# A recurrent layer with sixteen experts: solve steps in batches of eight tiles, gram products nine tiles ahead

## The chip, the core and the metric

The kernel runs on one core of one Trainium2 chip. The metric is the device time of one launch in microseconds. The engines are TensorE (PE: matmuls, written to PSUM), VectorE (DVE), ScalarE (ACT), GpSimd (POOL) and SyncE (SP), which here issues all DMAs. Each engine works through its own queue in order and waits for others by semaphores.

## What is computed

The input x is 8 sequences of 1024 steps of 256 numbers. Two branches work on the normalized input and are multiplied:

```python
xn = _layernorm(x, axis=-1)
# s: W is updated step by step, all 8 sequences together
def step(W, inp):
    xt, vt = inp                       # vt = xt @ Wkv[d:].T + bkv[d:]
    y = xt @ W.T
    gW = scale * ((y - vt).T @ xt)     # scale = 2 / (b * d)
    return (W - eta * gW, y)
# f: 16 experts, the gates of the best 6, made to sum to one
for e in range(E):
    out = out + x @ expert_w[e] * gate[:, e:e + 1]
x = x + s * _silu(f)
```

## The kernel before

A **tile** is 16 time steps of 8 sequences, 128 rows; there are 64 tiles (NT). Within a tile the recurrence is solved at once: with the products of all rows with each other (the gram matrix), masked and scaled into a triangular matrix a, the kernel finds u, the inverse of a unit triangular matrix, and so the errors of all rows against the state at the tile's start. Then the state W goes to the next tile. All large products are float32 numbers split into a high and a low part, three matmuls each (`accumulate`, L242 on); `split` (L142) makes the parts, the high one on ScalarE (L143), the low one on VectorE or GpSimd (L144).

Per tile i these functions run:

- `load` and `layernorm`: x comes by DMA; st, mv (VectorE), ve, rstd (GpSimd), then xn: on ScalarE with a shift for the first 8 tiles (`BY_ACT`, L206), on VectorE after that (L208). From tile 4 on a transposed copy is made by 32x32 blocks (xr, L214), written to a DRAM tile (`bounce`) and read back by four DMAs as xT.
- `transpose_x`: splits xT into xT_two (L235 on) and xn into xn_hi and xn_lo (L238 to L240).
- `project` and `project_end`: the gram products (two matmuls at L256, the copy cross on ScalarE at L262, and one more at L274, which adds the transposed cross part), and vr, the target values and router logits together (six matmuls). Of these come xx and a (L279, L280), lg (L269) and hv (L282).
- `gates`, for a group of tiles: the best six of sixteen logits, and the gates.
- `solve_0` to `solve_6`, for a group of tiles: small matmuls of 32x32 and 64x64 for all tiles of the group, with copies between them on VectorE and ScalarE. `solve_0` makes q1 on VectorE (L414). Then come six steps on TensorE, each of which needs the results of the one before: q and uq (L402), z (L440, L444), y (L458), z2 (L473), y2 (L484). At the end u is split into u_hi and u_lo.
- `errors_1`, `errors_2`, `update`: the recurrence of tile i, in order: pe with the state wt, p and its parts, pe with u, step, then wt_ps and the next state.
- `experts`, for each of eight pairs of experts: six matmuls of 512 columns into h (three PSUM buffers), and the weighted sum: for six experts (`ON_ACT`) on ScalarE and GpSimd (part, L554; mix, L557), for the rest on VectorE (mix, L563, L565). `finish` multiplies the branches and sends the tile out.

The order on TensorE and SyncE is written out by hand (`manual_schedule`); a scheduler places the instructions of the others. The main loop goes over 64 tiles and eight pairs each: a pair slot is numbered 8 i + pair, and `events` (L610 on) lists what is put ahead of the expert matmuls of each slot. Tiles are grouped 1, 1, 2, and then by four (`counts`, L89); a group serves for gates and solve steps both. With f the first slot of a group's first tile, its solve steps stand at f-10, f-8, f-6, f-4, f-2 and f (L635). Gram and vr of tile i stand at 8 (i - 5) + 1 (`AHEAD`), their ends one slot later, the first tiles earlier by a list (`preps`, L638). `errors_2` stands at 8 i + 3, `update` at 8 i + 5, or + 6 for every fourth tile (L622).

Of the kernel before, what the change touches and what calls it, by code (L numbers as in the profile page):

```python
# [36 lines left out]
P = 128  # L37
# [6 lines left out]
GROUP = 4  # L44
AHEAD = 5
BY_PE = 4
BY_ACT = 8
# [4 lines left out]
def ttt_moe_kernel(  # L52
# [26 lines left out]
    prep = ctx.enter_context(tc.tile_pool(name="prep", bufs=AHEAD + 1))  # L79
# [13 lines left out]
    for n, c in enumerate(counts):  # L93
        where += [(n, sum(counts[:n]), j) for j in range(c)]

# [27 lines left out]
    r_raw = const.tile([NE, D], F32)  # L123
    nc.sync.dma_start(out=r_raw, in_=router_w)
    w_raw = const.tile([P, 2 * KD, D], F32)
# [65 lines left out]
    def layernorm(i):  # L191
# [10 lines left out]
        q.xn = work.tile([P, D], F32, tag="xn", name=f"xn_{i}", bufs=3)  # L202
# [10 lines left out]
        xr = work.tile([P, D], F32, tag="xr", name=f"xr_{i}")  # L213
# [12 lines left out]
    def transpose_x(i):  # L226
        q = tiles[i]
        q.xT_two = prep.tile([P, KD, 2, P], F32R, tag="xT_two", name=f"xT_two_{i}")
        q.xT_hi, q.xT_lo = q.xT_two[:, :, 0, :], q.xT_two[:, :, 1, :]
        if i < BY_PE:  # L230
            t = misc(f"xtr_{i}")
            for k in range(KD):
                nc.tensor.transpose(t[:, k * P : (k + 1) * P], q.xn[:, k * P : (k + 1) * P], ident)
            split(q.xT_hi, q.xT_lo, t[:, : KD * P].rearrange("p (k t) -> p k t", k=KD))
        else:  # L235
            hi, lo = (a.rearrange("p k (b t) -> p k b t", b=NQ) for a in (q.xT_hi, q.xT_lo))
            split(hi, lo, q.xT.rearrange("p (b k t) -> p k b t", b=NQ, k=KD))
        q.xn_hi = prep.tile([P, D], F32R, tag="xn_hi", name=f"xn_hi_{i}")  # L238
        q.xn_lo = prep.tile([P, D], F32R, tag="xn_lo", name=f"xn_lo_{i}")
        split(q.xn_hi, q.xn_lo, q.xn, nc.gpsimd)  # L240
# [10 lines left out]
    def project(i, g, j):  # L251
# [10 lines left out]
        nc.scalar.copy(q.cross, gram[:, P : 2 * P])  # L262
        vr = misc(f"vr_{i}")
# [6 lines left out]
        q.vr = vr  # L270

    def project_end(i, g, j):
        q = tiles[i]
        nc.tensor.matmul(  # L274
            q.gram[:, :P], lhsT=q.cross, rhs=ident_r, start=False, stop=True, skip_group_check=True
        )
        xx = work.tile([P, P], F32, tag="xx", name=f"xx_{i}")
        with tc.high_priority() if j == g.count - 1 else nullcontext():
            nc.vector.tensor_add(xx, q.gram[:, :P], q.cross.bitcast(F32))  # L279
            nc.vector.tensor_mul(g.a[:, j, :, :], xx.unsqueeze(1).broadcast_to([P, 2, P]), masks)  # L280
        q.hv = prep.tile([P, D], F32, tag="hv", name=f"hv_{i}")
        nc.vector.scalar_tensor_tensor(  # L282
            q.hv, q.vr[:, :D], -0.5, half_b, op0=ALU.mult, op1=ALU.subtract
        )
# [15 lines left out]
    ones = const.tile([P, P], F32)  # L300
    nc.gpsimd.memset(ones, 1.0)
    keep = const.tile([P, 2, P], F32)
# [12 lines left out]
    u_full, t_half = [], []  # L315
    for n in range(2):
        u = const.tile([P, GROUP, P], F32, tag=f"u_{n}", name=f"u_{n}")
        nc.gpsimd.memset(u, 0.0)
        u_full.append(u)
        t = const.tile([P, GROUP // 2, P // 2], F32, tag=f"t_{n}", name=f"t_{n}")  # L320
        nc.gpsimd.memset(t, 0.0)
        t_half.append(t)

    stores = {}

    def open_group(n, first, count):
        m, j = first // GROUP, first % GROUP
        if j == 0:
            store = stores[m] = Prepared()
            store.a = group.tile([P, GROUP, 2, P], F32, tag="a", name=f"a_{m}")  # L330
            store.lg = group.tile([P, GROUP, NE + 2], F32, tag="lg", name=f"lg_{m}")
            nc.gpsimd.memset(store.lg[:, :, NE:], ABSENT)
            store.u, store.t = u_full[m % 2], t_half[m % 2]
            store.u_hi = group.tile([P, GROUP, P], F32R, tag="u_hi", name=f"u_hi_{m}")
            store.u_lo = group.tile([P, GROUP, P], F32R, tag="u_lo", name=f"u_lo_{m}")
            for name in ("q1", "q2", "uq", "tq", "z"):
                setattr(store, name, group.tile([P, GROUP, Q], F32, tag=name, name=f"{name}_{m}", bufs=1))
            store.z2 = group.tile([P, GROUP // 2, P // 2], F32, tag="z2", name=f"z2_{m}", bufs=1)
        g = Prepared()
        g.n, g.first, g.count = n, first, count  # L340
        for name, t in vars(stores[m]).items():
            if name in ("t", "z2"):
                setattr(g, name, t)
            else:
                setattr(g, name, t[:, j : j + count])
# [6 lines left out]
        g.half_of = [((j + n) % 2, (j + n) // 2) for n in range(count)]  # L352
        return g

    def gates(g):
# [35 lines left out]
        for j in range(c):  # L391
            q = tiles[g.first + j]
            q.gate, q.eps_sum = gate[:, j, :], eps_sum[:, j : j + 1]
            q.u_hi, q.u_lo = g.u_hi[:, j, :], g.u_lo[:, j, :]

    def step_q(g, name, rhs, out):
# [3 lines left out]
        for j in range(c):  # L400
            for b in range(P // Q):
                nc.tensor.matmul(  # L402
                    ps[at(b), j * Q : (j + 1) * Q], lhsT=g.a[at(b), j, 0, at(b)],
# [7 lines left out]
    def solve_0(g):  # L411
        c = g.count
        for b in range(P // Q):
            nc.vector.tensor_add(  # L414
                g.q1[at(b)], g.a[at(b), :, 1, at(b)],
                ident_q[at(b), :].unsqueeze(1).broadcast_to([Q, c, Q]),
# [17 lines left out]
    def solve_3(g):  # L434
        c = g.count
        ps = solving(f"z_ps_{g.n}")
        for j in range(c):
            o = slice(j * Q, (j + 1) * Q)
            for a, b in ((0, 1), (2, 3)):
                nc.tensor.matmul(  # L440
                    ps[at(a), o], lhsT=g.a[at(b), j, 0, at(a)], rhs=g.uq[at(b), j, :],
# [3 lines left out]
                ps[at(1), o], lhsT=g.a[at(0), j, 1, at(1)], rhs=g.tq[at(0), j, :],  # L445
# [24 lines left out]
    def solve_5(g):  # L470
        ps = solving(f"z2_ps_{g.n}").rearrange("p (m h) -> p m h", h=H)
        for j, (odd, m) in enumerate(g.half_of):
            nc.tensor.matmul(  # L473
                ps[at(odd, H), m, :], lhsT=g.a[H:, j, 0, :H], rhs=g.u[H:, j, H:],
                start=True, stop=True, skip_group_check=True,
            )
        for odd, js, ms in [(None, None, slice(0, g.count // 2))] if g.count == GROUP else g.halves:
# [3 lines left out]
    def solve_6(g):  # L481
# [8 lines left out]
        split(g.u_hi, g.u_lo, g.u)  # L490
# [4 lines left out]
    def errors_1(i):  # L495
# [8 lines left out]
        q.p = work.tile([P, D], F32, tag="p", name=f"p_{i}")  # L504
# [3 lines left out]
        q.p_hi = work.tile([P, D], F32R, tag="p_hi", name=f"p_hi_{i}")  # L508
        q.p_lo = work.tile([P, D], F32R, tag="p_lo", name=f"p_lo_{i}")
        split(q.p_hi, q.p_lo, q.p)  # L510

    def errors_2(i):
# [3 lines left out]
        q.step_hi = work.tile([P, D], F32R, tag="step_hi", name=f"step_hi_{i}")  # L516
        nc.scalar.mul(q.step_hi, e, neg_c)  # L517
        q.step_lo = work.tile([P, D], F32R, tag="step_lo", name=f"step_lo_{i}")
# [3 lines left out]
        q.hy = work.tile([P, D], F32, tag="hy", name=f"hy_{i}")  # L522
# [47 lines left out]
    def finish(i):  # L570
# [9 lines left out]
        o = work.tile([P, D], F32, tag="o", name=f"o_{i}")  # L580
# [7 lines left out]
    opened = {}  # L588
# [10 lines left out]
    def project_y(i):  # L599
        n, first, j = where[i]  # L600
        project_end(i, opened[n], j)
        if j == counts[n] - 1:
            with tc.high_priority():
                solve_0(opened[n])

    def solve_x(n, m):
        solve[m](opened[n])
# [25 lines left out]
    for n, c in enumerate(counts):  # L633
        f = 8 * sum(counts[:n])
        spots = solves.get(n, (f - 10, f - 8, f - 6, f - 4, f - 2, f))  # L635
        for m, spot in enumerate(spots):
            put(spot // 8, spot % 8, solve_x, n, m)
    preps = {1: 6, 2: 10, 3: 12, 4: 17, 5: 19, 6: 25, 7: 27, 8: 33, 9: 35}  # L638
    for i in range(1, NT):
        spot = preps.get(i, 8 * (i - AHEAD) + 1)  # L640
        norm, turn = {1: (1, 4), 2: (7, 9), 3: (8, 8)}.get(i, (spot - 10, spot - 1))
        fetch = max(4, spot - 21)
        if i >= BY_PE:
# [3 lines left out]
        put(spot // 8, spot % 8, project_x, i)  # L647
        put((spot + 1) // 8, (spot + 1) % 8, project_y, i)
# [3 lines left out]
    transpose_x(0)  # L652
    split_experts(0)
    load(1)
    for e in range(4, NE):
# [3 lines left out]
        if e in (9, 11):  # L659
            load(2 if e == 9 else 3)  # L660
    project_x(0)
    project_y(0)
# [41 lines left out]
```

## Time and profile before

| | us |
|---|---|
| median of 3 runs | 998.58 (998.12 to 998.90) |
| span of the profiled execution, first to last instruction | 997.4 |
| mean granted TensorE clock | 0.995 |
| TensorE busy | 974.0 |
| VectorE busy | 770.1 |
| GpSimd busy | 444.4 |
| ScalarE busy | 438.2 |

The profile is of one execution, whose own time the page gives as the span alone. A row of the timeline gives the start and the length of an instruction or of a merged run, the engine, the line, what it writes and reads, and how many (x). Matmuls overlap, so the length of one is more than the distance to the next; distances are read from starts. A float32 matmul that isn't split (the small ones of the solve steps) leaves two records. A row by stage gives for each engine the busy time and, behind it in brackets, the instructions; then the clock granted to TensorE, the share of the DMA engines and GB/s.

### The profile page before, as it was taken

What the parts mean: (1) busy time and instruction counts of PE and PEld (TensorE: products, weight loads), DVE (VectorE), ACT (ScalarE), POOL (GpSimd) and SP (SyncE); (2) the same over time, 40 slices, a digit from 0 to 9 for tenths busy, and PEclk for the clock granted to TensorE, in tenths of its full rate; (3) what the DMA queues carried; (4) which work ended last, traced back from release to release, by engine and by line L of the source; (5) the groups of instructions that cost most, each with busy time, mean ns of one, the idle gap of its engine ahead of it and who ended that gap; (6) DMA issues with size and microseconds to landing.
All of it is one profiled execution on the core that took longest, in us unless ns stands there. A gap on an engine that the chain in (4) does not pass through costs nothing.

```text
span 997.4 us, 19643 instructions
## 1 busy us (share of the span) xinstructions
PE 974.0 (98%) x6672; PEld 799.4 (80%) x6672; DVE 770.1 (77%) x2225; ACT 438.2 (44%) x1182; POOL 444.4 (45%) x677
## 2 busy tenths in 40 slices
PE   5899999999999999999999999999999999999997
PEld 4678888888888888888888888888888888888785
DVE  6878796877878778796877878778797777877664
ACT  6544444353443534444353443534444353443432
POOL 6633444444345344444444345344444444344343
PEclk9899999999999999999999999999999999999999
DMA  8021111111111111111111111111111111110000
GB/s 238 15 62 38 39 26 44 39 26 43 39 28 43 38 28 43 38 28 43 38 28 43 38 28 43 30 36 44 38 28 43 38 28 43 33 28 12 12 12 11
DMA packets 67092, 38.65 MB, mean 39 GB/s; under 512 B 38176, under 2 KB 66992, under 8 KB 66992
## 3 DMA queue, kind: packets, MB, share of 16 engines
q1 hardware_dynamic: 66992, 37.41, 13.8%
q8 instruction: 52, 0.85, 0.4%
q14 instruction: 48, 0.39, 0.1%
HBM read 21.13 MB, written 16.25 MB: 37 GB/s over the span
## 4 chain that ended last, share of the span: by engine, by line
PE 91%; DVE 3%; ACT 2%; issue 1%; POOL 1%; DMA 1%; SPq 0%; POOLq 0%; DVEq 0%; ACTq 0%
PE h L247 70%; PE pe L247 6%; PE wt_ps L247 5%; PE vr L247 5%; PE gram L256 2%; PE gram L274 1%; DVE q L414 1%; PE q_ps L402 1%; PE z_ps L473 1%; PE y_ps L484 1%; PE y_ps L458 1%; DVE mix L565 1%; PE uq_ps L402 1%; PE z_ps L440 0%; DMA eta_sb<-in_L_attn_eta_dram 0%
## 5 line engine op out<-in xcount | busy, mean ns | idle before, releaser
L247 PE MATMUL h<-we,xT_two 128*128 128x512 f32 x3072 | 784.8, 401 | 4.5 <-DVE mix L565 2.7
L247 PEld LDWEIGHTS h<-we,xT_two 128*128 128x128 f32 x3072 | 553.6, 188 | 121.0 <-issue 2.9
L565 DVE SCALAR_TENSOR_TENSOR mix<-h,gate,mix 128x256 f32<-128x256 f32 x576 | 265.8, 476 | 96.4 <-PE h L247 67.2
L554 ACT ACTIVATE part<-h,gate 128x256 f32<-128x256 f32 x384 | 181.9, 474 | 302.5 <-DVE mix L565 153.9
L557 POOL TENSOR_TENSOR mix<-mix,part 128x256 f32<-128x256 f32 x256 | 189.5, 740 | 115.7 <-ACT part L554 104.7
L579 POOL TENSOR_TENSOR my<-m,hy 128x256 f32<-128x256 f32 x64 | 47.6, 744 | 161.0 <-DVE m L575 157.6
L557 POOL TENSOR_TENSOR mix<-part,part 128x256 f32<-128x256 f32 x64 | 49.9, 780 | 74.0 <-ACT part L554 74.0
L582 POOL TENSOR_TENSOR o<-o,x 128x256 f32<-128x256 f32 x63 | 46.4, 737 | 67.7 <-DVE lg L269 58.0
L195 DVE BATCH_NORM_STATS2 st<-x 128x6 f32<-128x256 f32 x64 | 27.0, 423 | 58.2 <-DMA x<-in_L_attn_x_dram 58.2
L199 POOL TENSOR_SCALAR ve<-mv 128x1 f32<-128x1 f32 x64 | 14.9, 234 | 100.6 <-DVE mv L197 67.9
L247 PE MATMUL vr<-w_vr,xT_two 128*128 128x272 f32 x384 | 59.1, 290 | 0.0
L144 DVE TENSOR_TENSOR wt_lo<-wt_ps,wt_hi 128x512 fp32r<-128x512 f32 x64 | 42.9, 670 | 21.0 <-ACT wt_hi L143 20.8
L143 ACT CAST p_hi<-p 128x256 fp32r<-128x256 f32 x64 | 26.0, 406 | 68.9 <-DVE p L505 68.7
L208 DVE TENSOR_SCALAR xn<-x,mv,rstd 128x256 f32<-128x256 f32 x56 | 45.2, 808 | 11.9 <-POOL rstd L201 11.8
L143 ACT CAST xT_two<-xT 128x256 fp32r<-128x256 f32 x60 | 24.4, 407 | 65.4 <-PE h L247 63.8
L247 PEld LDWEIGHTS vr<-w_vr,xT_two 128*128 128x128 f32 x384 | 52.3, 191 | 0.0
L517 ACT ACTIVATE step_hi<-pe,neg_c 128x256 fp32r<-128x256 f32 x64 | 30.3, 474 | 46.3 <-PE pe L247 46.0
L144 POOL TENSOR_TENSOR xn_lo<-xn,xn_hi 128x256 fp32r<-128x256 f32 x64 | 47.8, 749 | 6.0 <-ACT xn_hi L143 5.4
L247 PEld LDWEIGHTS pe<-wt_hi,xT_two 128*128 128x128 f32 x256 | 39.2, 188 | 5.8
L144 DVE TENSOR_TENSOR p_lo<-p,p_hi 128x256 fp32r<-128x256 f32 x64 | 40.4, 631 | 0.8 <-ACT p_hi L143 0.4
L247 PE MATMUL pe<-wt_hi,xT_two 128*128 128x256 f32 x256 | 40.7, 281 | 0.0
L143 ACT CAST wt_hi<-wt_ps 128x512 fp32r<-128x512 f32 x64 | 37.1, 580 | 6.8 <-PE wt_ps L247 6.4
(117 smaller groups left out, 1197.6 us busy)
## 6 DMA issues: line engine op xcount, KB each, us to landing
x<-in_L_attn_x_dram SPq DMA_DIRECT2D x64, 128.0 KB, 2.7
out_dram<-o SPq DMA_DIRECT2D x64, 128.0 KB, 2.3
bounce<-xr SPq DMA_DIRECT2D x60, 128.0 KB, 2.3
xT<-bounce SPq DMA_DIRECT2D x240, 32.0 KB, 1.8
raw<-in_L_ffn_expert_w_dram SPq DMA_DIRECT2D x16, 256.0 KB, 5.2
w_raw<-in_L_attn_Wkv_dram SPq DMA_DIRECT2D x1, 256.0 KB, 2.7
w_raw<-in_L_attn_W_dram SPq DMA_DIRECT2D x1, 256.0 KB, 5.1
bias<-in_L_attn_bkv_dram SPq DMA_DIRECT2D x1, 128.0 KB, 4.8
```

The source lines that it names most:

```text
L143: nc.scalar.copy(hi, src)
L144: (engine or nc.vector).tensor_sub(lo, src, hi.bitcast(F32))
L195: nc.vector.bn_stats(st, xt)
L208: nc.vector.tensor_scalar(q.xn, xt, mv[:, 0:1], rstd, ALU.subtract, ALU.mult)
L247: nc.tensor.matmul(o, lhsT=a, rhs=b, start=first and m == 0, stop=(m == len(terms) - 1), **kw)
L256: nc.tensor.matmul(gram[:, : 2 * P], lhsT=q.xT_hi[:, k, :], rhs=q.xT_two[:, k, :, :].rearrange("p n t -> p (n t)"), start=(k == 0), stop=( ...
L517: nc.scalar.mul(q.step_hi, e, neg_c)
L554: nc.scalar.mul(part, he, gate)
L557: nc.gpsimd.tensor_add(new, q.mix[1], part)
L565: nc.vector.scalar_tensor_tensor(new, he, gate, q.mix[j], op0=ALU.mult, op1=ALU.add)
L579: nc.gpsimd.tensor_mul(my, m, q.hy)
L582: (nc.vector if i == NT - 1 else nc.gpsimd).tensor_add(o, o, xt)
```

## The change

Gates stay with the groups of four. The solve steps get batches of their own: 1, 1, 2, 4, 4, 4, then six of eight tiles. The gram products leave `project` and become `products`, which stands nine tiles ahead (`FAR`) instead of five; vr stays at five. The splitting of xn leaves `transpose_x` and becomes `split_x`, two tiles ahead of its update. ScalarE normalizes the first 24 tiles instead of 8. Buffers are counted anew: more for xn (10) and xT_two (11), three groups' worth of a, and single buffers for p, p_hi, p_lo, step_hi, step_lo, hy, xr, xx, u_hi, u_lo and the u that the steps build; some constants of the start share buffers with later tiles, and o is made in place of my. With f the first slot of a batch's first tile, the steps of a batch of eight stand at f-11, f-9, f-7, f-5, f-3 and f-1.

```diff
+BATCH = 8
 AHEAD = 5
+FAR = 9
-BY_ACT = 8
+BY_ACT = 24
...
-    prep = ctx.enter_context(tc.tile_pool(name="prep", bufs=AHEAD + 1))
+    prep = ctx.enter_context(tc.tile_pool(name="prep", bufs=FAR + 2))
...
+    batches = [1, 1, 2, 4, 4, 4]
+    while sum(batches) < NT:
+        batches.append(min(BATCH, NT - sum(batches)))
...
+    def split_x(i):
+        q = tiles[i]
+        q.xn_hi = prep.tile([P, D], F32R, tag="xn_hi", name=f"xn_hi_{i}", bufs=3)
+        q.xn_lo = prep.tile([P, D], F32R, tag="xn_lo", name=f"xn_lo_{i}", bufs=3)
         split(q.xn_hi, q.xn_lo, q.xn, nc.gpsimd)
...
+    u_full = const.tile([P, BATCH, P], F32)
+    nc.gpsimd.memset(u_full, 0.0)
...
-    def solve_0(g):
-        c = g.count
+    def solve_0(g, lo, hi):
+        first = (g.first + lo) % GROUP
+        a = grams[(g.first + lo) // GROUP][:, first : first + hi - lo]
         for b in range(P // Q):
             nc.vector.tensor_add(
-                g.q1[at(b)], g.a[at(b), :, 1, at(b)],
-                ident_q[at(b), :].unsqueeze(1).broadcast_to([Q, c, Q]),
+                g.q1[at(b), lo:hi], a[at(b), :, 1, at(b)],
+                ident_q[at(b), :].unsqueeze(1).broadcast_to([Q, hi - lo, Q]),
             )
...
-        split(g.u_hi, g.u_lo, g.u)
...
+        for lo, hi in g.parts:
+            split(u_hi[:, lo:hi], u_lo[:, lo:hi], g.u[:, lo:hi])
...
+    def products_x(i):
+        products(i)
+
+    def products_y(i):
+        n, first, j = which[i]
+        last = j == batches[n] - 1
+        products_end(i, gram_of(i), last)
+        if n not in started:
+            started[n] = open_batch(n, first, batches[n])
+        if last or j % GROUP == GROUP - 1:
+            with tc.high_priority():
+                solve_0(started[n], j // GROUP * GROUP, j + 1)
...
-    for n, c in enumerate(counts):
-        f = 8 * sum(counts[:n])
-        spots = solves.get(n, (f - 10, f - 8, f - 6, f - 4, f - 2, f))
+    for n, c in enumerate(batches):
+        f = 8 * sum(batches[:n])
+        spots = solves.get(n, [f - 11 + 2 * m if c > GROUP else f - 10 + 2 * m for m in range(len(solve))])
...
-    preps = {1: 6, 2: 10, 3: 12, 4: 17, 5: 19, 6: 25, 7: 27, 8: 33, 9: 35}
+    preps = {1: 6, 2: 10, 3: 12, 4: 17, 5: 19, 6: 25, 7: 27, 8: 33, 9: 35, 10: 41, 11: 49}
     for i in range(1, NT):
-        spot = preps.get(i, 8 * (i - AHEAD) + 1)
+        near = preps.get(i, 8 * (i - AHEAD) + 1)
+        spot = preps.get(i, 8 * (i - FAR) + 1)
+        if 11 < i < 23:
+            spot = 49 + (i - 11) * 16 // 3
         norm, turn = {1: (1, 4), 2: (7, 9), 3: (8, 8)}.get(i, (spot - 10, spot - 1))
         fetch = max(4, spot - 21)
+        apart = max(turn, 8 * (i - 2) + 6)
...
-        put(spot // 8, spot % 8, project_x, i)
-        put((spot + 1) // 8, (spot + 1) % 8, project_y, i)
+        put(apart // 8, apart % 8, split_x, i)
+        put(spot // 8, spot % 8, products_x, i)
+        put(near // 8, near % 8, project_x, i)
+        put((spot + 1) // 8, (spot + 1) % 8, products_y, i)
```

## The prediction

> **What bounds the kernel now.** I read the page first: busy shares, the row of slices, the chain. Then the busy time by stage, then the timeline of TensorE over one group of four tiles.
>
> ```profile
> PE 974.0 (98%) x6672; PEld 799.4 (80%) x6672; DVE 770.1 (77%) x2225; ACT 438.2 (44%) x1182; POOL 444.4 (45%) x677
> ...
> PE   5899999999999999999999999999999999999997
> ...
> PEclk9899999999999999999999999999999999999999
> ...
> PE 91%; DVE 3%; ACT 2%; issue 1%; POOL 1%; DMA 1%; SPq 0%; POOLq 0%; DVEq 0%; ACTq 0%
> ```
>
> TensorE is busy 98% of the span and carries 91% of the chain that ended last; no other engine is above 77%. By stage:
>
> ```profile
> 0.00:20.00 20.00, 10.51 (x55) 7.84 (x56) 12.16 (x38) 12.30 (x28) 12.11 (x26) 1.00 0.87 258
> 20.00:60.00 40.00, 34.63 (x203) 26.39 (x202) 33.30 (x123) 22.52 (x70) 23.26 (x36) 0.91 0.18 50
> 60.00:120.00 60.00, 58.38 (x458) 47.53 (x457) 48.83 (x150) 28.77 (x87) 23.84 (x38) 1.00 0.14 37
> 180.00:900.00 720.00, 719.92 (x4997) 594.40 (x4997) 567.40 (x1630) 313.00 (x840) 322.17 (x489) 1.00 0.13 36
> ```
>
> From 180 to 900 us TensorE (first pair of numbers after the length) is idle 0.08 us in 720. So in the steady part the time is the sum of TensorE's start-to-start distances, and a change matters there only if it alters that sum or makes TensorE wait. Idle time of TensorE lies in the first 120 us (9.5 + 5.4 + 1.6 us), 0.4 us in the next 60, and 6.5 us at the end.
>
> The sum is read from the timeline of TensorE (start, length with overlap, records):
>
> ```profile
> 500.40 0.28 PE L247 MATMUL wt_ps<-step_lo,xn_hi 128*128 128x256 f32 x1
> 500.61 0.45 PE L402 MATMUL q_ps<-q,a 32*32 32x32 f32 x32
> 500.99 3.06 PE L247 MATMUL h<-we,xT_two 128*128 128x512 f32 x12
> 503.89 0.64 PE L247 MATMUL pe<-wt_hi,xT_two 128*128 128x256 f32 x4
> 504.37 0.40 PE L247 MATMUL pe<-wt_lo,xT_two 128*128 128x256 f32 x2
> 504.70 0.45 PE L402 MATMUL uq_ps<-q,a 32*32 32x32 f32 x32
> 505.08 1.67 PE L247 MATMUL h<-we,xT_two 128*128 128x512 f32 x6
> 506.59 0.40 PE L256 MATMUL gram<-xT_two 128*128 128x256 f32 x2
> ```
>
> Full-size matmuls have fixed distances: eighteen h take 4.22 us (484.99 to 489.21), 0.234 each; a 256-column one takes 0.12 (500.28 to 500.40). What departs from that stands at each solve step. Take the first step, q: wt_ps began at 500.40 and should have handed over at 500.52, but q began at 500.61 (0.09 lost). From q's first start to the next h are 0.38. The twelve h behind it take 2.90 to pe, where 12 x 0.234 = 2.81 (another 0.09). The step costs 0.56 us, of which the small matmuls themselves are the 0.45 less the last one's 0.19, plus one distance: 0.27. **0.29 us is the price of entering and leaving small matmuls**, however many there are.
>
> The same reading of the other five steps of this group: uq 0.57 (of it matmuls 0.27), z 0.57 (0.26), y 0.55 (0.27), z2 0.54 (0.27), y2 0.57 (0.27). Sum 3.36 us a group, 1.61 of it matmuls and **1.75 fixed**.
>
> **The change, part by part.**
>
> *Batches of eight.* The number of small matmuls stays: the compiled order holds as many TensorE instructions of each kind as before. Groups were 1, 1, 2 and fifteen of 4: 18. Batches are 1, 1, 2, three of 4 and six of 8: 12. Six groups' worth of entries go: 6 x 1.75 = **-10.5 us**. A batch of eight needs twice the small matmuls in a row, so I need their cost to be linear. An early two-tile step bears on that:
>
> ```profile
> 61.73 0.33 PE L402 MATMUL uq_ps<-q,a 32*32 32x32 f32 x16
> 61.99 0.50 PE L256 MATMUL gram<-xT_two 128*128 128x256 f32 x2
> ```
>
> With 16 records it is 0.26 to the next start instead of 0.38 with 32: 0.12 for 16 records, 0.0075 each, and the rest does not shrink. 64 records were not seen. The bounds are: cost proportional to tiles, nothing saved (0); second half free, 6 x 3.36 = -20.2. I take the linear value, which two sizes show.
>
> The trace shows starts 0.0075 to 0.0085 us apart within a step. The Trainium skill, "TensorE: Matmul & The Clock Gate", section "Wait — 56ns, not 53.3ns?", speaks against the gain: starts never come closer than about 25 ns however small the matmul. By that floor the four steps with 24 or 32 records would be all streaming and nothing fixed; only z2 and y2 with 8 records would keep some 0.35 each (0.54 and 0.57 less 8 x 0.025), and the saving would be an estimated 6 x 0.71 = 4.3 us. This trace goes below the floor, so the measured distance decides.
>
> *Gram nine tiles ahead, vr five ahead.* The gram matmuls (L256, L274) leave their vr matmuls, one each per tile as before. Full-size kinds follow one another at their own distances whatever the order, so moving them costs nothing. L274 after h costs what it costs after z (from the start before L274 to the second h behind it: 0.58 after h, mean of 37 places; 0.60 after z, mean of 12). 0 us.
>
> *Waits in the steady part.* TensorE waits for nothing now; does it after? Each step has two pair slots to the next, as before, but the eight-tile forms are longer. Two places are tight. First, q: its last gram product stands at slot f-14 as before, but q moves from f-10 to f-11. What lay between and now lies behind is six h (1.41) and the update (0.71): 2.12 us less time. On VectorE:
>
> ```profile
> 496.05 2.13 DVE L414 TENSOR_TENSOR q<-a,ident_q 32x128 f32<-32x128 f32 x4
> ```
>
> It ends at 498.18, q begins at 500.61: 2.43 us spare. Over the thirteen steady groups I read 2.07 to 2.60, so -0.05 to 0.48 remain, and VectorE's order around it is as before (behind the mix of pair 1 and pair 2). Wait: 0 to 0.1 us a batch. Behind a waiting q_ps the whole of TensorE's queue stands, so any wait there counts in full.
>
> Second, from y to z2: ScalarE's copies of u and t end 0.9 to 1.7 us before z2 now. Afterwards y stands directly behind errors_2, so step_hi (L517, 0.47) runs ahead of the copies, and these grow: u 0.175, 0.202, 0.249 for 1, 2, 4 tiles, hence about 0.34 for 8; t 0.176, 0.202, hence about 0.25; together 2 x 0.09 + 2 x 0.05 = 0.28. The results come 0.27 later, the longer row of matmuls and the update lengthen the distance from 4.09 to 4.37. 0.1 to 0.9 us are left. From uq to z similarly 1.1 to 1.6 now, less 0.27 and less 0.29 (VectorE's uq and tq for 256 columns): 0.5 to 1.0. I put down +0.4 us for all six batches, bounds 0 and 6 x 0.3 = 1.8.
>
> *The denser stage.* Products of tiles 12 to 22 come every 5.33 pair slots instead of 8, in slots 6 to 14. Each tile brings VectorE 3.0 us (st 0.42, mv 0.17, xr 0.44, xT_two 0.41, xx 0.28, a 0.46, its share of q 0.5, shift 0.28) apart from xn. VectorE does 47.5 us in 60 now, 11.9 a slot. Without xn (0.81) and with shift (0.28) and half a tile more (1.5) it is 12.8 a slot, some 51 of 60. ScalarE takes 1.5 x 0.60 for xn and half a tile of the rest, about 1.3 on 6.5 a slot: over half busy. On SyncE's queue the x load, the bounce and its four reads keep their order within a tile and come half as often again per slot; the next xr must wait for the bounce of the last (2.3 us to landing, 5 slots of 1.4 us apart), so that is covered. step_lo ends 0.3 to 1.0 us before the update needs it in most slots, so a few waits are likely. +0.6 us, bounds 0 and +5 (0.5 in each of nine slots).
>
> *The start.* split_x (L143 0.41 on ScalarE, L144 0.75 on GpSimd) moves from the products to two tiles before the update, out of the crowded first slots for tiles 2 to 7; VectorE's order of mixes and gates there changes. TensorE's idle time from 20 to 120 us is 7.0 us, so at best -7. I take 0, bounds -2.5 and +2.5 (a third of it), as one wait is likely traded for another: h waits 2.95 us at 38 us for buffers, and gate work now stands later there.
>
> *Buffers.* One buffer instead of two for p, p_hi, step_hi, hy, xx, xr, u_hi: each old tile's last reader comes at least two pair slots before the next write, so 0. The memsets of u (0.53 each) lie in the loading phase: 0. The end keeps its tail of 6.5 us.
>
> **Sum.** -10.5 + 0.4 + 0.6 + 0 = -9.5 us. The profiled execution has a span of 997.4; the median of the runs is 998.58, 1.2 above it. From the median: **989.1 us**.
>
> **Rivals.**
>
> *A: the batches gain, the edges give half back.* With the dense stage and the start at their upper bounds it is 998.6 - 10.5 + 0.4 + 5 + 2.5 = 996.0; half of both gives 992.3. For: spare times of 0.3 us, and VectorE at 85% in those slots. Against: it is at 79% now and nothing waits.
>
> *B: slower, because q waits in every batch.* If the four q additions fall behind one more mix of h on VectorE (pair 3's), they end 1.4 us later and q waits 1.1: 6 x 1.1 = 6.7, still 996. Behind pair 4's mix it is 2.5 us: 6 x 2.5 = 15, 989.1 + 15 = 1004. It decides from 1.7 us a batch on. For: 2.12 of the 2.4 us spare are used up. Against: VectorE's order as compiled has them ahead of both mixes.
>
> *C: nothing is saved,* because the fixed part grows with the batch (the 0 bound): 998.6 + 0.4 + 0.6 = 999.6. For: no row shows 64 records. Against: 16 and 32 do.
>
> **Chances.** Forecast 0.68, A 0.16, B 0.09, C 0.07. Forecast's own range: 989.1 - 2.5 (start) - 1.0 (no waits) = 985.6, put at 985.3, to 989.1 + 2.5 = 991.6. Eight in ten reaches into A: 985.3 to 995.0. About 0.2% (2 us) can be told from no change: faster 0.85 (forecast, A, a little of B and C), same 0.07, slower 0.08.
>
> **What would show it.** In the timeline of TensorE a q step of 64 records should take about 0.65 us to the next h, and eight steady tiles some 118.0 us instead of 2 x 59.88. TensorE's busy time from 240 to 900 should stay at 100%; idle time with VectorE's L414 equivalent as releaser would be B, idle time between 60 and 220 us A. A step of 64 records near 0.76 us with late h behind it would be C.

## The result: slower by 0.34%

| | before | after |
|---|---|---|
| median of six runs, us | 998.09 (997.77 to 998.90) | 1001.69 (1000.18 to 1003.00) |
| ratio after to before | | 1.0034, interval 1.0022 to 1.0045 |
| span of the profiled execution, us | 997.4 | 999.6 |
| mean granted TensorE clock | 0.995 | 0.997 |

The forecast was 989.1 us (985.3 to 995.0). The page of after, its busy time and the chain that ended last:

```profile
PE 965.9 (97%) x6672; PEld 796.4 (80%) x6672; DVE 763.0 (76%) x2207; ACT 427.6 (43%) x1101; POOL 442.1 (44%) x675
...
PEclk9999999999999999999999999999999999999999
...
PE 53%; DVE 21%; DMA 8%; issue 5%; POOL 5%; ACT 5%; SPq 3%; POOLq 0%; DVEq 0%; ACTq 0%
```

TensorE is busy 8.1 us less than before, so something was saved, but the span is 2.2 longer: it is idle 10.3 us more. In the chain TensorE falls from 91% to 53%, and VectorE has 21%: results arrive late now. Where, the rows by stage say (start and end, length, then TensorE's busy time first):

```profile
0.00:20.00 20.00, 8.83 (x33) 6.77 (x33) 10.75 (x26) 12.73 (x28) 12.78 (x25) 1.00 0.86 246
20.00:60.00 40.00, 37.67 (x253) 28.76 (x254) 37.22 (x149) 24.47 (x74) 22.05 (x35) 0.96 0.21 56
60.00:120.00 60.00, 59.29 (x447) 48.54 (x445) 46.44 (x146) 29.37 (x89) 23.37 (x37) 1.00 0.16 43
120.00:180.00 60.00, 57.13 (x402) 46.59 (x401) 47.01 (x143) 28.17 (x76) 26.24 (x42) 1.00 0.17 45
180.00:300.00 120.00, 116.80 (x928) 94.43 (x927) 91.32 (x276) 55.00 (x147) 52.62 (x82) 1.00 0.15 41
300.00:900.00 600.00, 593.00 (x4163) 493.96 (x4162) 467.71 (x1322) 245.25 (x618) 264.50 (x401) 1.00 0.13 34
```

Idle time (length less busy time), after less before: +1.7, -3.0 and -0.9 in the first three rows, together -2.3; +2.5 from 120 to 180 (2.87 against 0.36); +3.2 from 180 to 300; and +7.0 from 300 to 900, where before had 0.03. The waits of TensorE from 300 to 900 us (total, times, longest):

```profile
PE gram L278 <- DVE hv L296: 5.2, 4, 1.3
PE h L259 <- ACT part L583: 0.8, 2, 0.5
PE z_ps L492 <- ACT t_half L485: 0.5, 1, 0.5
```

Four times, 120 us apart (396.9, 517.4, 637.4 and 757.9), so once for every eight tiles, TensorE waits 1.3 us at L278, the last gram product (L274 in before). It reads cross, which ScalarE copies. TensorE's timeline of one of these places, then ScalarE's, then three rows of VectorE's:

```profile
508.13 0.75 PE L420 MATMUL uq_ps<-q,a 32*32 32x32 f32 x64
508.81 1.67 PE L259 MATMUL h<-we,xT_two 128*128 128x512 f32 x6
...
514.28 0.40 PE L268 MATMUL gram<-xT_two 128*128 128x256 f32 x2
514.52 1.56 PE L259 MATMUL h<-we,xT_two 128*128 128x512 f32 x6
517.40 0.33 PE L278 MATMUL gram<-ident_r,cross 128*128 128x128 f32 x1 [1.31 <-DVE hv L296]
```

```profile
512.06 1.65 ACT L448 COPY u_full<-uq 32x256 f32<-32x256 f32 x4 [1.57 <-DVE uq L424]
513.72 1.22 ACT L451 COPY t_half<-tq 32x128 f32<-32x128 f32 x4
514.97 0.41 ACT L152 CAST xT_two<-xT 128x256 fp32r<-128x256 f32 x1
...
517.09 0.26 ACT L274 CAST cross<-gram 128x128 fp32r<-128x128 f32 x1
```

```profile
510.22 0.69 DVE L153 TENSOR_TENSOR wt_lo<-wt_ps,wt_hi 128x512 fp32r<-128x512 f32 x1 [1.08 <-ACT wt_hi L152]
...
511.61 0.41 DVE L424 TENSOR_TENSOR uq<-uq_ps,ident_q 128x256 f32<-128x256 f32 x1
...
515.40 0.42 DVE L153 TENSOR_TENSOR xT_two<-xT,xT_two 128x256 fp32r<-128x256 f32 x1 [1.48 <-ACT xT_two L152]
```

uq's matmuls begin at 508.13, but VectorE first waits 1.08 us for wt_hi (wt_hi starts on ScalarE at 509.61, behind a part that had to wait for VectorE, 3.1 us behind the last wt_ps matmul; in before it is 0.6), then makes wt_lo and two mixes, and adds uq up only at 511.61. Eight copies of u and t follow on ScalarE and take 2.9 us. Behind them in its queue stand the high part of xT_two (514.97), for which VectorE waits 1.48 us, and much later cross (517.09), which ends at 517.35; L278 begins at 517.40. Between the two, VectorE's mixes are late by its wait, and ScalarE waits for one of them in turn (0.46 us, ahead of the part at 516.71). So the delay goes from ScalarE to VectorE and back. The row names hv (VectorE) as releaser, the weight load of L278 names cross:

```profile
PEld gram L278 <- ACT cross L274: 11.6, 11, 1.7
```

hv ends at 517.36 and the trace has a wait for VectorE at this place too, so it doesn't tell which of the two ended last; both stand behind the same copies. The tile that is split at 514.97 isn't the one whose gram stands here: in after every xT_two is complete at least 8.4 us before its own gram starts (in before 0.05 at the least), so xT_two counts here only by VectorE's wait. In before the same engine had this order:

```profile
504.09 0.41 ACT L143 CAST xT_two<-xT 128x256 fp32r<-128x256 f32 x1 [1.15 <-PE h L247]
...
506.62 1.20 ACT L429 COPY u<-uq 32x128 f32<-32x128 f32 x4
507.84 1.01 ACT L432 COPY t<-tq 32x64 f32<-32x64 f32 x4
508.87 0.27 ACT L262 CAST cross<-gram 128x128 fp32r<-128x128 f32 x1
```

There xT_two went first, the copies were 2.2 us, and cross ended at 509.14 against L274's start at 509.45.

Idle time is not the whole of it. From the first h of one tile to that of the tile 32 further on (tiles 16 and 48, 1536 h each) are 478.99 us in before (from 281.96), 481.00 in after (from 289.76), and 471.58 in e16 below (from 285.44), which has the batches and almost no wait: 9.4 us lost in after over four waits, some 2.4 each.

### The profile page after: what moved, and what is told of

The parts are those of the page before. It is cut to its first block, busy times and chain, and to the rows that moved or that the text cites. A ratio compares the mean times of both kernels' runs of the same rounds, so it can differ in the third digit from the quotient of the medians.

```text
span 999.6 us, 19616 instructions
## 1 busy us (share of the span) xinstructions
PE 965.9 (97%) x6672; PEld 796.4 (80%) x6672; DVE 763.0 (76%) x2207; ACT 427.6 (43%) x1101; POOL 442.1 (44%) x675
## 4 chain that ended last, share of the span: by engine, by line
PE 53%; DVE 21%; DMA 8%; issue 5%; POOL 5%; ACT 5%; SPq 3%; POOLq 0%; DVEq 0%; ACTq 0%
PE h L259 41%; DVE mix L594 5%; DMA x<-in_L_attn_x_dram 5%; PE pe L259 4%; PE vr L259 3%; ACT part L583 3%; PE wt_ps L259 2%; POOL mix L586 2%; DVE q L433 2%; DMA bounce<-xr 1%; DVE mix L592 1%; DVE wt_lo L153 1%; SPq L230 1%; POOL rstd L210 1%; DMA raw<-in_L_ffn_expert_w_dram 1%
## 5 line engine op out<-in xcount | busy, mean ns | idle before, releaser
L611 POOL TENSOR_TENSOR my<-my,x 128x256 f32<-128x256 f32 x63 | 46.5, 738 | 73.1 <-DVE top L387 25.9
L259 PEld LDWEIGHTS vr<-w_vr,xT_two 128*128 128x128 f32 x384 | 55.7, 191 | 4.3
L217 DVE TENSOR_SCALAR xn<-x,mv,rstd 128x256 f32<-128x256 f32 x40 | 32.8, 819 | 15.6 <-POOL rstd L210 15.2
L153 DVE TENSOR_TENSOR p_lo<-p,p_hi 128x256 fp32r<-128x256 f32 x64 | 42.5, 664 | 2.5 <-ACT p_hi L152 1.1
L548 DVE SCALAR_TENSOR_TENSOR step_lo<-pe,neg_c,step_hi 128x256 fp32r<-128x256 f32 x64 | 30.4, 475 | 13.5 <-ACT step_hi L546 13.5
```

The source lines that it names most:

```text
L153: (engine or nc.vector).tensor_sub(lo, src, hi.bitcast(F32))
L217: nc.vector.tensor_scalar(q.xn, xt, mv[:, 0:1], rstd, ALU.subtract, ALU.mult)
L259: nc.tensor.matmul(o, lhsT=a, rhs=b, start=first and m == 0, stop=(m == len(terms) - 1), **kw)
L548: nc.vector.scalar_tensor_tensor(q.step_lo, e, neg_c, q.step_hi.bitcast(F32), op0=ALU.mult, op1=ALU.subtract)
L611: (nc.vector if i == NT - 1 else nc.gpsimd).tensor_add(o, o, xt)
```

## The experiments

In the expectations, theory 1 says that the eight copies stand ahead of cross in ScalarE's queue and make L278 alone late (its rival in e2 is gram's own place, behind vr and so with less cover ahead of L278); theory 2 in the x load, which stands behind out on SyncE and holds up st, step_lo and the rest of VectorE's queue; theory 3 in the steps, which stand one pair slot earlier (f-11). Theories R, F and P are about the dense stage, 3a and 3b are two forms of theory 3. Every ratio is against the kernel before on the same chip. The chips differ: before took 998.09 to 999.25 us on them. So the third column has each median less that of before on its own chip, and what is said below to be above or below another run is the difference of two such figures; after has +3.60.

| run | median, us | to before, us | ratio and interval |
|---|---|---|---|
| e1 L278 two slots later | 1005.83 | +6.70 | 1.0066, 1.0054 to 1.0078 |
| e2 gram ahead of vr | 1000.25 | +1.12 | 1.0013, 1.0004 to 1.0021 |
| e3 BY_ACT 8 | 1004.94 | +5.81 | 1.0055, 1.0043 to 1.0067 |
| e4 batches of four | 1012.48 | +13.35 | 1.0129, 1.0116 to 1.0142 |
| e5 x load earlier | 1010.47 | +11.95 | 1.0121, 1.0108 to 1.0135 |
| e6 e5 and e1 | 1012.12 | +13.60 | 1.0131, 1.0117 to 1.0145 |
| e7 steps at f-10 | 994.88 | -3.64 | 0.9963, 0.9951 to 0.9976 |
| e8 two buffers for xr | 999.47 | +0.95 | 1.0007, 0.9998 to 1.0016 |
| e9 e7 and e2 | 995.59 | -2.60 | 0.9972, 0.9960 to 0.9983 |
| e10 e7, slower ramp | 997.87 | -0.32 | 0.9998, 0.9989 to 1.0007 |
| e11 e7, e2, e8, slower ramp | 996.72 | -1.47 | 0.9983, 0.9974 to 0.9992 |
| e12 before, steps at f-11 | 1024.12 | +25.93 | 1.0273, 1.0251 to 1.0294 |
| e13 copies of u and t on GpSimd | 990.77 | -7.96 | 0.9919, 0.9907 to 0.9931 |
| e14 e7, other pair slots | 994.92 | -3.81 | 0.9962, 0.9949 to 0.9976 |
| e15 e14 and e13 | 989.18 | -9.55 | 0.9903, 0.9890 to 0.9917 |
| e16 e7 and e13 | 988.96 | -9.77 | 0.9902, 0.9888 to 0.9915 |
| e17 before, copies on GpSimd | 1000.08 | +0.83 | 1.0009, 1.0000 to 1.0018 |
| e18 e12, copies on GpSimd | 1009.58 | +10.33 | 1.0104, 1.0090 to 1.0118 |

**e1.** For the first tile of each batch of eight, L278 and what follows it stand two slots later.

```diff
-        put((spot + 1) // 8, (spot + 1) % 8, products_y, i)
+        end = spot + (3 if i > 23 and i % 8 == 0 else 1)
+        put(end // 8, end % 8, products_y, i)
```

> Theory 1 (ScalarE's queue): in the slot where a batch's u and t are copied, eight lengthened copies (2.87 us) stand ahead of the copy cross, and L278 on TensorE waits 1.2 to 1.48 us for it, five times. Putting only those five L278 two pair slots later takes the waits away: about 7 us less, some 994.5 us. Rival (VectorE and ScalarE are as a whole behind in that slot): the wait moves on to the next reader (pe with u, or h for its buffer), less than 2 us gained, some 1000.

1005.83, 3.1 us above after. L278's waits are gone from 300 us on, but two others took their place. The waits of TensorE in e1:

```profile
PE wt_ps L259 <- DVE step_lo L548: 4.7, 6, 1.2
...
PE z_ps L492 <- ACT t_half L485: 3.3, 6, 0.7
```

The late results are late for everything behind them; L278 is only the first to ask. Theory 1 falls in this form.

**e2.** Within a slot, gram stands ahead of the vr of another tile, which gives cross six matmuls (0.75 us) more time.

```diff
         put(spot // 8, spot % 8, products_x, i)
-        put(near // 8, near % 8, project_x, i)
         put((spot + 1) // 8, (spot + 1) % 8, products_y, i)
+    for i in range(1, NT):
+        near = preps.get(i, 8 * (i - AHEAD) + 1)
+        put(near // 8, near % 8, project_x, i)
```

> Order of vr and gram in their common pair slot swapped back (gram first), all else as after the change. If L278 waits because gram now ends 0.75 us later, each of its five waits gets 0.75 shorter: 3.7 us less, 998. Theory 1 (the queue of copies ahead of cross decides, not gram): no change within 1 us, 1001.5.

1000.25, 2.5 below after. L278 starts 1.40 us behind the last h where it was 1.71 (0.24 is due): 0.3 of 0.75 gained. So what is short is not only the cover of the gram; what stands ahead of cross in ScalarE's queue is the larger part.

**e3.** ScalarE normalizes eight tiles instead of 24.

```diff
-BY_ACT = 24
+BY_ACT = 8
```

> ScalarE normalizes 8 tiles again instead of 24. If ScalarE is the engine that is late in slots 6 to 14 (about 5 us of waits from 120 to 182 us), they shrink: 3 us less, 998.5. If VectorE is, xn there (0.81 us a tile) adds to it: 2 to 5 us more, 1004 to 1007. After 300 us nothing changes by either.

1004.94, 2.2 above after: giving xn back to VectorE makes it worse. This part of the change helps.

**e4.** Batches of four, all else as in after.

```diff
-BATCH = 8
+BATCH = 4
```

> BATCH = 4, so solve steps in fours at the places of before, while gram stays nine tiles ahead and the dense stage stays. Entry theory: 36 entries more, 10.8 us more, and the waits that belong to batches of eight (about 3 us to 300 us, 5.8 after) go: 1003.6. If the waits belong to the gram's new place and not to the batches, they stay: 1012.

1012.48, 9.8 above after. That is about the entries of six batches (10.5), and the waits at L278 do not shrink in sum (7.3 us in after):

```profile
PE gram L278 <- ACT cross L274: 7.2, 11, 0.9
```

The steps of a batch of four stand at f-10, as in before, yet nearly every group waits at L278, about half as long. So the length of a batch alone does not make the wait. There cross again stands behind the copies (2.2 us), and gram itself, behind vr, comes 0.75 us later than in before.

**e5 and e6.** The x load goes four slots earlier on SyncE, ahead of out; e6 adds the edit of e1.

```diff
-        fetch = max(4, spot - 21)
+        fetch = max(4, spot - 25)
```

> The x load moves from behind the out DMA to ahead of it in SyncE's queue (pair slot 0 instead of 4 of the same tile); all else as after the change. Theory 2 (a late out holds up x, x holds up st on VectorE, and step_lo stands behind st): VectorE's waits of st for x (41 us) shrink below 15 us and the waits of wt_ps and z2 after the update go, but L278 still waits 1.2 to 1.5 us per batch: 1.5 to 3 us less, 999.5. Theory 1 (only cross on ScalarE): no change, 1001.5.

> Both edits: the five L278 two pair slots later, and x ahead of out on SyncE. Theory 2: with x there in time nothing takes the place of L278's wait, so about 1.5 us a batch goes in five batches: 7 to 9 us less than after the change, 993 to 995. Rival (VectorE and ScalarE simply have too much to do in these two slots): the wait only moves again, 1000 or more.

1010.47 and 1012.12: worse. VectorE's waits for x were to fall below 15 us and grew from 41.0 to 48.6 in e5, and xr waits 32.4 us in 29 places for the bounce to release its buffer (in after 7.5 in six). So the edit didn't bring x in time, and theory 2 is left open as a part of the delay; a cure it is not.

**e7.** The steps of a batch of eight stand where those of before stood.

```diff
-        spots = solves.get(n, [f - 11 + 2 * m if c > GROUP else f - 10 + 2 * m for m in range(len(solve))])
+        spots = solves.get(n, [f - 10 + 2 * m for m in range(len(solve))])
```

> The steps of a batch of eight at f-10 to f, as groups had, instead of f-11 to f-1; all else as after the change. Theory 3 (the steps come one pair slot too early for VectorE: q additions and uq stand in the slot of the gates): the waits of q and of pe for wt_lo (0.25 and 0.2 us a batch) go, uq is added at once, and L278 of the next slot waits only for the copies, 0.5 us or less: 6 us less, 995.5. Theory 1: the copies now stand one pair slot nearer to cross, L278 waits longer: 1003.

994.88, 7.2 below after, and faster than before. ScalarE's timeline in the same place:

```profile
507.40 0.41 ACT L152 CAST xT_two<-xT 128x256 fp32r<-128x256 f32 x1 [1.03 <-PE h L259]
...
510.06 1.66 ACT L448 COPY u_full<-uq 32x256 f32<-32x256 f32 x4
511.73 1.22 ACT L451 COPY t_half<-tq 32x128 f32<-32x128 f32 x4
...
513.35 0.26 ACT L274 CAST cross<-gram 128x128 fp32r<-128x128 f32 x1
```

xT_two is ahead of the copies again, by 2.7 us, and VectorE no longer waits for it. Cross, still behind them, ends at 513.61, and L278 waits 0.29 us. One pair slot is worth 7.2 us. e7 does not tell which engine's queue does it, since both VectorE's and ScalarE's orders change.

**e8.** Two buffers for xr (and two for xT instead of three, for room).

```diff
-        q.xT = work.tile([P, KD * P], F32, tag="xT", name=f"xT_{i}", bufs=3)
+        q.xT = work.tile([P, KD * P], F32, tag="xT", name=f"xT_{i}", bufs=2)
-        xr = work.tile([P, D], F32, tag="xr", name=f"xr_{i}", bufs=1)
+        xr = work.tile([P, D], F32, tag="xr", name=f"xr_{i}", bufs=2)
```

> Two buffers for xr again (and two instead of three for xT, to make room). The profile after the change shows VectorE waiting 7.5 us in six places for a bounce to release the single xr, all in the dense stage. If these waits make wt_lo late there (1.7 us at 144 us, 0.8 at 138, 0.7 at 124), most of the 4 us from 120 to 182 us go: 998. If VectorE's amount of work does, 1001.

999.47, 2.7 below after. But in its profile (an execution of 1000.68) TensorE's idle time stays as it was, 2.99 us from 120 to 180, 3.13 from 180 to 300 and 6.85 from 300 to 900 (2.87, 3.20 and 7.00 in after). A single xr may have a small price; where it lies these profiles don't show.

**e9.** The edits of e7 and e2 together.

> The six steps at f-10 to f as in e7, and within a slot the gram products stand ahead of the vr products of another tile, so that cross has six 272-column matmuls more before L278 needs it. Theory 3 (steps in VectorE's heaviest slot cause the steady waits; what e7 left at L278, 0.36 to 0.63 in three places and less elsewhere, is gram's short cover): what the order gave in e2, 0.3 us in each of five batches, is given here too, as far as a wait is left: 994.9 - 1.5 = 993.4, and L278 has no wait above 0.3. Rival (the waits left in e7 come from ScalarE's queue of copies alone): 994.5 to 995.5, L278 waits as in e7.

995.59, no gain over e7 (the intervals overlap); L278 waits 2.0 us in five places, against 2.3 in e7. From 300 us on it waits 0.7 where it was 1.2, but z now waits 0.7 for t_half, a copy of ScalarE's too. The rival holds: what e7 left there is ScalarE's queue.

**e10.** e7 with a slower ramp, and one batch more.

```diff
-    batches = [1, 1, 2, 4, 4, 4]
+    batches = [1, 1, 2, 4, 4, 4, 4, 4]
...
-        if 11 < i < 23:
-            spot = 49 + (i - 11) * 16 // 3
+        if 11 < i < 31:
+            spot = 49 + (i - 11) * 32 // 5
```

> The steps at f-10 to f as in e7, and the gram products of tiles 12 to 30 come every 6.4 slots instead of those of 12 to 22 every 5.33, so the first batch of eight is that at tile 24 and there is one batch more (13 instead of 12): one more entry of six steps, +1.75. Theory R (the waits of 120 to 205 us come from the rate of the products, VectorE having half a tile more in every slot): of the 4 to 5 us there most goes, and of the 3.1 at 257 to 283 some moves on: 994.9 + 1.75 - 4 = 992.6, waits from 120 to 205 below 1.5. Rival F (they come from something that the ramp's rate does not change, such as xn on ScalarE, single buffers or nine tiles' distance): 994.9 + 1.75 = 996.6, waits of 120 to 205 as in e7.

997.87, 3.3 above e7, of which one entry is 1.75. The waits move to other places (at 175, 186, 238, 316 us) and don't go: a lower rate of the products is no cure.

**e11.** The edits of e7, e2, e8 and e10 together.

> All together: steps at f-10 to f, gram ahead of vr, products of tiles 12 to 30 every 6.4 slots, and two buffers for xr (with two instead of three for xT). If the gains add: 994.9 - 1.5 (order, e2) + 1.75 - 4 (ramp) - 2 (xr, e8) = 989 at best; if order and ramp are worth what the rivals say, 994 to 996.6. Below 993.7 it is the fastest of the versions run.

996.72: the gains don't add.

**e12.** The kernel before, and this one edit.

```diff
-        spots = solves.get(n, (f - 10, f - 8, f - 6, f - 4, f - 2, f))
+        spots = solves.get(n, (f - 11, f - 9, f - 7, f - 5, f - 3, f - 1))
```

> The kernel before with one edit: the six solve steps of its groups of four stand one pair slot earlier, at f-11, f-9, f-7, f-5, f-3, f-1. Nothing else of the change is in it. Theory 3 (the slot is the cause): uq's additions fall behind wt_lo and the mixes of VectorE's heaviest slot here as well, and what stands behind them on ScalarE is late: with the 0.5 to 1.1 us a group that the step of five batches (6.8 us between after and e7) suggests for the shorter forms, 14 groups give +7 to +15, 1006 to 1014. Rival (only the forms of eight tiles are long enough to be late): 998 to 1000.5, no wait above 0.3 us from 300 to 900 us.

1024.12: 25.9 us for one slot, far beyond what theory 3 had expected. The waits of TensorE, and a timeline of ScalarE:

```profile
PE gram L256 <- DVE xT_two L144: 23.3, 14, 2.0
```

```profile
580.38 1.22 ACT L429 COPY u<-uq 32x128 f32<-32x128 f32 x4 [1.44 <-DVE uq L406]
581.62 1.00 ACT L432 COPY t<-tq 32x64 f32<-32x64 f32 x4
582.65 0.40 ACT L143 CAST xT_two<-xT 128x256 fp32r<-128x256 f32 x1
```

This is the cleanest form of the fault. With the steps a slot earlier the compiled order has the copies ahead of xT_two; gram, which reads xT_two a slot later, waits up to 2.0 us, 14 times. In after gram doesn't wait for its xT_two, which is complete 8.4 us or more ahead; there the loss comes by VectorE's wait and cross, appears at L278 instead, and is smaller.

**e13.** The kernel after, steps at f-11, but the copies of u and t go to GpSimd.

```diff
-            nc.scalar.copy(g.u[at(b), :, at(b)], g.uq[at(b)])
+            nc.gpsimd.tensor_copy(g.u[at(b), :, at(b)], g.uq[at(b)])
...
-                nc.scalar.copy(g.t[at(2 * odd + b), ms, at(b)], g.tq[at(b), js])
+                nc.gpsimd.tensor_copy(g.t[at(2 * odd + b), ms, at(b)], g.tq[at(b), js])
```

> The kernel after, steps at f-11, but the copies of u and t behind uq (8 for a batch) go to GpSimd instead of ScalarE. Theory 3a (ScalarE's 2.9 us of copies stand ahead of xT_two's high part and of cross in its queue): L278's waits of 1.3 us fall below 0.3, about 1.4 us in each of six batches, 1001.7 - 8 = 994. Theory 3b (uq's late additions on VectorE hold up the rest by themselves): cross and z stay late, 1000 to 1002, or above if GpSimd is slower at copies than ScalarE.

990.77, 11.6 below after, and further down than theory 3a had it (994). The timelines of VectorE, GpSimd and ScalarE in the same place of the batch:

```profile
506.03 0.42 DVE L424 TENSOR_TENSOR uq<-uq_ps,ident_q 128x256 f32<-128x256 f32 x1
```

```profile
506.51 1.80 POOL L448 COPY u_full<-uq 32x256 f32<-32x256 f32 x4 [0.78 <-DVE uq L424]
508.37 1.62 POOL L451 COPY t_half<-tq 32x128 f32<-32x128 f32 x4
```

```profile
505.06 0.41 ACT L152 CAST xT_two<-xT 128x256 fp32r<-128x256 f32 x1
...
509.88 0.27 ACT L274 CAST cross<-gram 128x128 fp32r<-128x128 f32 x1
```

uq is added where it stood in VectorE's order in after, behind wt_lo and two mixes, and as late: 3.35 us behind the start of its matmuls (502.68), 3.48 in after. GpSimd takes 3.4 us for the copies where ScalarE took 2.9. Still the waits at L278 from 300 us on are gone, as ScalarE splits xT_two 1.5 us ahead of the copies instead of behind them, and VectorE doesn't wait for it. So it is the copies' place in ScalarE's queue (theory 3a), not uq's lateness. The Trainium skill, "PSUM — Partial Sum Buffer", section "Engine vs sequencer instructions", states that the queues of ScalarE, VectorE and GpSimd are strictly first in, first out; the runs agree: xT_two starts 0.03 us behind the last of the copies in after (514.94 and 514.97), and from uq's start on VectorE to cross's start on ScalarE are 5.5 us in after (511.61 to 517.09), with the copies between, and 3.9 here (506.03 to 509.88).

**e14.** e7 with the same rate in the dense stage, but products in pair slots 3, 1, 1 instead of 6, 3, 1.

```diff
-            spot = 49 + (i - 11) * 16 // 3
+            spot = 49 + (2, 8, 16)[i % 3] + 16 * (i // 3 - 4)
```

> Steps at f-10 to f as in e7; the dense stage has the same rate (three tiles in two outer passes), but its products stand in pair slots 3, 1, 1, 3, 1, 1 and so on instead of 6, 3, 1, 6, 3, 1, so that no tile's normalization, transpose and split stand beside the update of pairs 5 and 6. Theory P (the place in the pass makes the waits of the dense stage): of the 4 to 5 us of 120 to 205 at least half goes, 992 to 993. Rival (the rate makes them, wherever they stand): 994.5 to 996.5.

994.92, as e7. Theory P falls.

**e15 and e16.** The copies on GpSimd together with e14, and with e7.

> Steps at f-10 to f, the pair slots of e14, and the copies of u and t on GpSimd. If both theories hold: 994.9 - 2 (place) - 1.5 (the 0.3 to 0.6 left at L278 in e7) = 991.4. If neither does: 995 to 997.

> Steps at f-10 to f, and the copies of u and t on GpSimd; the dense stage as in after. Theory 3a: the rest of L278's waits in e7 (2.3 us) goes, 992.5 to 993.5. Theory 3b: 994.5 to 996.

989.18 and 988.96: the fastest two, 0.98% below before, and not to be told apart. The row from 180 to 900 us, first of e7, then of e13, then of e16 (before had 719.92, after 709.80):

```profile
180.00:900.00 720.00, 715.46 (x5133) 596.47 (x5132) 566.62 (x1611) 301.66 (x768) 321.09 (x486) 1.00 0.13 35
```

```profile
180.00:900.00 720.00, 717.41 (x5146) 597.85 (x5146) 566.65 (x1615) 284.76 (x715) 342.45 (x544) 1.00 0.13 35
```

```profile
180.00:900.00 720.00, 718.58 (x5159) 600.72 (x5159) 569.06 (x1615) 285.50 (x716) 345.15 (x546) 1.00 0.13 35
```

TensorE's idle time there is 10.2 us in after, 4.5 in e7, 2.6 in e13 and 1.4 in e16.

**e17 and e18.** The edit of e13 in the kernel before, and in e12.

> The kernel before, its groups of four and its steps as they were; the copies of u and t behind uq go to GpSimd. If these copies only hurt where xT_two or cross stand behind them: before has no wait of TensorE there (0.08 us idle from 180 to 900), so 998 to 999, and batches of eight with the copies out of the way are worth 989.0 - 998.5 = -9.5, against the -10.5 + 1.0 that the sum had. Rival (the copies cost before something too): 994 to 997, and the batches are worth 5 to 8.

> e12 (before, steps at f-11 to f-1) with the copies of u and t on GpSimd. Theory 3a: gram no longer waits for xT_two, and of the 25.9 us nearly all goes, 998 to 1001. Theory 3b (uq's late additions hold up xT_two on VectorE): at least 10 us stay, above 1008.

e17: 1000.08, no gain. Before had nothing late behind the copies, so they cost it nothing, and the 9.8 us of e16 belong to the change, not to the copies' new place by itself. e18: 1009.58. Of e12's 25.9 us 15.6 go; 10.3 stay, just what theory 3b had set as its mark (at least 10), so in groups of four theory 3a is the larger part and not the whole. What stays comes late on VectorE, where wt_lo in turn waits for ScalarE:

```profile
570.51 0.69 DVE L144 TENSOR_TENSOR wt_lo<-wt_ps,wt_hi 128x512 fp32r<-128x512 f32 x1 [1.08 <-ACT wt_hi L143]
571.12 0.86 DVE L565 SCALAR_TENSOR_TENSOR mix<-h,gate,mix 128x256 f32<-128x256 f32 x2
571.91 0.28 DVE L406 TENSOR_TENSOR uq<-uq_ps,ident_q 128x128 f32<-128x128 f32 x1
572.22 0.31 DVE L425 STREAM_TRANSPOSE tq<-uq 128x128 f32<-128x128 f32 x1
572.46 0.83 DVE L565 SCALAR_TENSOR_TENSOR mix<-h,gate,mix 128x256 f32<-128x256 f32 x2
573.21 0.41 DVE L144 TENSOR_TENSOR xT_two<-xT,xT_two 128x256 fp32r<-128x256 f32 x1
```

wt_hi starts 2.8 us behind the last wt_ps matmul here (569.90 and 567.14), as in after; the copies' new place doesn't change that. wt_lo ends at 571.20 and its matmuls start at 571.26, 0.62 us behind the wt_hi matmuls instead of 0.48; xT_two ends at 573.62 and gram starts at 573.67. A few tenths a group at each, in 14 groups, are of the size of the rest; that they are all of it was not tried.

## Why the prediction was wrong, point by point

- **Batches of eight, -10.5: right.** In after's timeline uq costs 0.68 us to the next h, and the six h behind it take 1.50 where 1.41 are due: with 0.08 lost at the entry 0.85 for eight tiles, against 0.57 for four. The working had 0.57 + 32 x 0.0075 = 0.81. Two batches of four would be 1.14, so 0.29 is saved a step. The sign that the prediction named, some 118.0 us for eight steady tiles, is met where the copies are out of the way: 117.9 in e16 (a quarter of the 471.58 above), beside 119.75 in before and 120.25 in after. So a batch saves 1.86 where 1.75 was forecast. That e16 as a whole is 9.8 below before, beside -9.5 forecast in all, is in part chance: it isn't the kernel of the forecast, and its idle time from 120 to 300 us is 2.3 above that of before, where 0.6 was put down. The floor of about 25 ns between starts (the Trainium skill, "TensorE: Matmul & The Clock Gate", section "Wait — 56ns, not 53.3ns?"), which the prediction set aside, doesn't appear with 64 records either: at 25 ns a record they would take 1.6 us, at 25 ns a matmul (two records each) 0.8, and the next h starts after 0.68. The prediction's 4.3 us by that floor took each record for a matmul.
- **Waits in the steady part, +0.4, bounds 0 to 1.8: the step that failed.** They were 7.0 us of TensorE's idle time from 300 to 900 us, and by the starts 2.4 us for each batch that waits (9.4 in 32 tiles), against 0.07 forecast and 0.3 at most. The step named two tight places, q and the way from y and uq to z2 and z, and read the copies' growth (0.28 us in all behind y) only as a delay of what reads them. What stands behind the copies in ScalarE's queue, xT_two and cross, was not read, nor that moving the steps by one slot turns the order of xT_two and the copies around. The cause is shown from two sides: one slot back alone (e7) gives 7.2, the copies elsewhere alone (e13) 11.6, and the slot alone in before (e12) costs 25.9, of which the copies are 15.6 (e18). How the other 10.3 divide, wt_hi's later place among them, is open.
- **Gram nine tiles ahead, 0: wrong in the same way.** The matmuls themselves cost nothing by moving, but gram now stands behind vr and L278 no longer has vr ahead of it: 0.75 us less for cross. Alone (e2) that is worth 2.5 us; e4, where batches are of four at f-10, shows the waits that go with it.
- **The denser stage, +0.6, bounds 0 to 5: too low, and for another reason.** Idle time rose by 2.5 us from 120 to 180 and by 3.2 from 180 to 300. Of both rows' 6.1 us in after, 2.1 are at L278 as in the steady part, and the copies on GpSimd (e13) take away 3.2. Neither a lower rate (e10) nor other pair slots (e14) helped, and two buffers for xr (e8) left these rows as they were. ScalarE's xn, costed as harmless, is a help (e3). In e16 2.7 us remain in these two rows, 1.5 of them one wait for wt_lo; what makes them is open.
- **The start, 0, bounds ±2.5: right in size.** Idle time in the first 120 us fell by 2.3.
- **Buffers, 0: not settled.** Two buffers for xr, with one less for xT, took 2.7 us less (e8), but no idle time went with them.
- **Rival B** had the right mechanism (a wait in every batch, from an in-order engine) and near the right size (2.5 us a batch for 1004) at the wrong place: q in place of cross, VectorE in place of ScalarE. The point in its disfavour, VectorE's order as compiled, was true and beside the matter.

The span's own account: busy time -8.1, idle time -2.3 + 2.5 + 3.2 + 7.0 = +10.4, together +2.3 beside the span's +2.2. The -8.1 is not the batches' saving alone: in e16 TensorE is busy 960.3 us, 13.7 less than in before, so some 5.6 us of after's waits are likely to stand in its busy time.

## What to carry to other kernels

A sum over start-to-start distances tells what a bound engine saves, and did so here to 0.1 us a batch; it says nothing about what comes late. When a step moves by a slot or grows, list for every in-order engine that serves it what stands behind its instructions in the compiled order, before and after, and not only who reads its results: an engine that is 43% busy cost this change its whole gain. When such a wait is cured by moving the waiting instruction (e1), it turns up at the next one in line; move what stands ahead of it, to an engine with idle time, if need be a slower one.

## What was not expected of the hardware

- 64 records of 32x32 matmuls in a row (32 matmuls) take 0.68 us to the next full-size matmul, 32 records 0.38: the small matmuls cost in proportion, about 0.009 us a record, and only the entry, some 0.29 us, is fixed.
- GpSimd's copies of 32x256 and 32x128 take 0.45 and 0.41 us each in the place shown (1.80 and 1.62 for four; 0.41 and 0.37 in the mean of all 24), against 0.41 and 0.31 on ScalarE (0.40 and 0.30): here the slower engine was the faster kernel.
- Idle time doesn't hold every wait. e18 has 9.1 us more span than e17, but from 300 to 900 us its TensorE is only 1.4 us less busy (598.54 against 599.93): the matmuls that come a few tenths late have longer records (0.50 instead of 0.40 for two gram matmuls), which count as busy. Distances between starts show them.
